# A mixture-of-experts gate in phases: two blocks in the last phase instead of four, three in the first instead of one

## The chip, the cores and the metric

The kernel runs on one core of a Trainium2 chip. The metric is the device time of one execution in microseconds (us). Engines are named as in the profile: PE (TensorE), DVE (VectorE), ACT (ScalarE), POOL (GpSimd), SP (SyncE, which here only issues DMAs). Each engine takes its instructions in order.

## What is computed

One layer of a graph network and one feed-forward layer, on 6250 nodes of 256 numbers, with 100,000 edges:

```
Wh    = layernorm(x) @ W + b, two heads of 128
e     = leaky_relu(s[src] + t[dst]), s and t linear in Wh
x     = x + softmax-weighted sum of Wh[dst] over the edges of each src
xf    = layernorm(x);  Hd = gelu(xf @ W1 + b1)              (1024 wide)
probs = softmax(Hd @ Wg + bg)                               (8 experts)
x     = x + max(probs) * (Hd @ Wd[argmax] + bd[argmax])
```

Every node uses the one expert that its gate finds likeliest.

## The kernel before

Nodes are worked in 49 blocks of 128 (the last, block 48, has 106). The first 105 us project the nodes, write their rows to a table in DRAM and sort the edges.

**The edge stage** then takes a block every three slots of a written-out plan. For each block POOL issues 15 gathers of 128 table rows (`fetch`, L800), in three parts of five; DVE weighs them (`weigh`, L832), ACT copies the weights (L833), PE sums them (`add_up`, L840), and `finish` divides, adds x and takes mean and variance. Before that, `window`, `measure`, `split`, `choose` and `spread` find the block's edges; `spread` sends a small table through DRAM (`lrow`, `lbc`) with two DMAs on SP.

**The gate stage** works on four blocks at a time, a phase. `blocks_of(k)` says which blocks phase k has: phase 0 has block 0, phase 1 blocks 1 to 4, and so on, to phase 12 with blocks 45 to 48. A phase is normed (`g_norm`, `g_xn`), turned (`g_turn`), taken through the hidden layer in four parts (`g_hidden`, L923, with Gelu on ACT, L925), the logits (`g_logits` L961, `g_logits_out` L967, `g_fold` L973), the softmax and choice on DVE (`g_bias`, `g_max`, `g_exp`, `g_choose`), a count on PE (`g_count`, L1020 and L1021) and the places on DVE (`g_place`). `g_rows` turns the hidden rows back (L1044, copied by ACT, L1045), `g_rest` adds the node's x and gate, and `g_send` has POOL scatter the block's rows of 1282 numbers into `by_expert` in DRAM, a list for each expert (L1066).

**The list stage** takes full tiles of 128 rows of one expert, called entries here. `tabulate` makes a table on DVE of which tiles they are; `w_load` has SP load one (L1132), `w_turn` turns it on PE (L1044 again), `w_expert` multiplies it by the expert's weights (L1150 for the bias, L1152), `w_out` scales and adds on DVE (L1166). The results of most phases are put off: `w_wait` writes them to DRAM, and at the end `late_load` (SP) and `late_send` (POOL, L1183) bring them to the output. Those of the last two phases go straight to the output (`w_send`, POOL, L1190). Phase 12 has 14 entries, 55 in all; 37 are put off. Lists that are read while later rows are still sent lag by 512 rows (`LAG`).

**What sets the order.** `at(slot, place, fn, ...)` puts a step into a plan; it is sorted by slot, then place, then order of entry, and the steps are emitted in that order under a manual schedule. So each engine's queue has the order of the plan. Block b has its slots around 3b, phase k starts at u[k] = 3 * (its last block) + 5: 137 for phase 11, 149 for phase 12. Waits are derived from the tiles that a step reads and writes; `by_expert` is one tensor, and a load of it waits for the scatters that come before it in the plan. Buffers come from pools: three PSUM buffers `pf`, four `row` buffers and four `wg` buffers in SBUF, which `room` lends to rows late in the run, two `y` buffers. `hT`, which holds the hidden rows of a phase, exists once. Nine fills of the lists with empty rows (L614) stand in the plan at slots 26, 38, ... 122.

Of the kernel before, what the change touches and what calls it, by code (L numbers as in the profile page):

```python
# [36 lines left out]
def common_path(  # L37
# [36 lines left out]
    NB = -(-N // P)  # L74
# [17 lines left out]
    TW = H * D2  # L92
    SE = D2 + D
    FB = 4
    NPH = -(-(NB - 1) // FB) + 1
    G = P // 4

    RW = C + 4
# [70 lines left out]
    def rows_of(b):  # L169
        return min(P, N - b * P)  # L170
# [16 lines left out]
    with ExitStack() as edges:  # L187
# [3 lines left out]
        def at(slot, place, fn, *args):  # L191
            plan.append((slot, place, len(plan), fn, args))
# [225 lines left out]
        def scales(b0, b1):  # L418


            n = b1 - b0
            r = rs[:, b0:b1]
            ve = sp.tile([P, NB], F32, name="n1ve")[:, :n]
            gi = sp.tile([P, NB], I32, name="n1gi")[:, :n]
            sq = sp.tile([P, NB], F32, name="n1sq")[:, :n]
            g = gi.bitcast(F32)
            yield nc.vector.tensor_scalar(ve, mv[:, b0:b1, 1], EPS, None, op0=ALU.add)
            yield nc.vector.tensor_single_scalar(gi, ve.bitcast(I32), 1, op=ALU.logical_shift_right)
            yield nc.vector.tensor_scalar(gi, gi, -1.0, float(0x5F375A00), op0=ALU.mult, op1=ALU.add)
            for it in range(3):  # L430
                yield nc.vector.tensor_mul(sq, g, g)
                yield nc.vector.scalar_tensor_tensor(sq, sq, -0.5, ve, op0=ALU.mult, op1=ALU.mult)
                yield nc.vector.scalar_tensor_tensor(r if it == 2 else g, sq, 1.5, g,
                                                     op0=ALU.add, op1=ALU.mult)
# [79 lines left out]
        for i, (d, flip) in enumerate(steps):  # L514
            t = 11 + 1.7 * i if i < 18 else 41.6 + 1.02 * (i - 18)
# [16 lines left out]
        for f0, f1, t0, step in ((n0, n1, 8.0, 0.7), (n4, NB - 1, 15, 2.0)):  # L532
            for j, b in enumerate(range(f0, f1)):
                c = b % CH
                t = t0 + step * (j - 0.5 * c)
# [7 lines left out]
        for c0, c1, t in ((0, n0, 0.27), (n0, n2, 15), (n2, n4, 31), (n4, NB, 58.5)):  # L543
            todo = scales(c0, c1)
            for i in range(12):
                early(t + (0.001 if c0 == 0 else 0.12) * i, next, todo, None)
        for b in range(NB):
            t = XN0 + NODE * b
# [67 lines left out]
        win, kept, rows, own, sums, res = {}, {}, {}, {}, {}, {}  # L616
# [226 lines left out]
        def finish(b):  # L843
            kept.pop(b)
            r = rows_of(b)
            k = -(-b // FB)
            i = b - blocks_of(k)[0]
            if i == 0:
                res[k] = {"rows": fw.tile([P, FB, RW], F32, name="res"),
                          "mom": fw.tile([P, FB, 2], F32, name="mom")}  # L850
                if blocks_of(k)[-1] == NB - 1 and N % P:
                    nc.vector.memset(res[k]["rows"], 0.0)
                    nc.vector.memset(res[k]["mom"], 0.0)
            o = res[k]["rows"][:r, i, :]
            xo = own.pop(b)[:r]
            p_a = sums.pop(b)
            den = ep.tile([P, H], F32, name="den")
            nc.vector.tensor_scalar(den_all[:r, b, :], p_a[:r, D:D2], TINY, None, op0=ALU.max)
            nc.vector.reciprocal(den[:r], den_all[:r, b, :])
            for h in range(H):  # L860
                hs = slice(h * D, (h + 1) * D)
                nc.vector.scalar_tensor_tensor(o[:, hs], p_a[:r, h * D2:h * D2 + D], den[:r, h:h + 1], xo[:, hs],
                                               op0=ALU.mult, op1=ALU.add)
            st = ep.tile([P, 6], F32, name="st2")
            nc.vector.bn_stats(st[:r], o[:, :C])
            nc.vector.bn_aggr(res[k]["mom"][:r, i, :], st[:r])
# [15 lines left out]
        put_off, late_y = [], {}  # L882
        put_off_idx = fc.tile([P, 2 * PAIRS], I32, name="put_off_idx")
# [41 lines left out]
                nc.scalar.activation(hT[:, j, :w], ph[:, :w], AF.Gelu, bias=wt["b1"][:, j:j + 1])  # L925

        def blocks_of(k):
            return range(max(0, (k - 1) * FB + 1), min(NB, k * FB + 1))

        def g_norm(k):  # L930
            bs = blocks_of(k)
# [108 lines left out]
        def turn_half(o, rows, h):  # L1040

            pT = pff.tile([P, 512], F32, name="pf")
            for j in range(4):
                nc.tensor.transpose(pT[:, j * P:(j + 1) * P], rows(4 * h + j), ident)  # L1044
            nc.scalar.copy(o, pT)  # L1045

        def room(late):

            if not late:
                return fw.tile([P, RD], F32, name="row", bufs=4)  # L1050
            return gp.tile([P, HT, TW], F32, name="wg").rearrange("p t c -> p (t c)")[:, :RD]

        def g_rows(k, i):

            row = res[k]["row", i] = room(k == NPH - 1 and i > 1)
            for h in range(2):
                turn_half(row[:, h * 512:(h + 1) * 512], lambda j: hT[:, j, i * P:(i + 1) * P], h)

# [68 lines left out]
        def w_load(k, i):  # L1127
            sr = res[k]["sr", i] = room(k == NPH - 1 or k == NPH - 2 and i in (2, 3))
            _, ro = nc.values_load_multi_w_load_instructions(
                res[k]["where"][0:1, i:i + 1], engines=[SP], min_val=0, max_val=SPARE,  # L1130
                skip_runtime_bounds_check_because="a tile of a list, or the spare tile")
            nc.sync.dma_start(out=sr, in_=by_expert[ds(ro[0], P), :])  # L1132
# [23 lines left out]

        def w_out(k, i):
            sr = res[k].pop(("sr", i))
            idx = res[k]["idx", i] = (put_off_idx[:, len(put_off):len(put_off) + 1] if k < NPH - 2 else
                                      fw.tile([P, 1], I32, name="idx"))  # L1160
            if "again" in res[k]:
                nc.vector.tensor_add(idx, sr[:, HID + C + 1:], res[k]["again"][:, i:i + 1])
            else:
                nc.vector.tensor_copy(idx, sr[:, HID + C + 1:])
            y = res[k]["y", i] = fw.tile([P, C], F32, name="y", bufs=2)
            nc.vector.scalar_tensor_tensor(y, res[k].pop(("py", i))[:, :C], sr[:, HID + C:HID + C + 1],  # L1166
                                           sr[:, HID:HID + C], op0=ALU.mult, op1=ALU.add)
# [28 lines left out]
        for b in range(NB):  # L1196
            u = 3 * b
# [27 lines left out]
        worked = n_off = 0  # L1225
        u = [3 * blocks_of(k)[-1] + 5 for k in range(NPH)]
        for k in range(NPH):
            bs = blocks_of(k)
            v = u[k]
            last = k == NPH - 1  # L1230
            at(v, 34 if last else 51, g_norm, k)
            for i in range(-(-len(bs) // 2)):
                at(v + 0.5 * i, 52, g_xn, k, i)
                at(v + 1, 38 + 0.1 * i, g_turn, k, i)
                at(v + 1, 45 + 0.1 * i, g_turned, k, i)
            for q in range(4):
                at(v + 2 + q, 20, g_hidden, k, q)
            at(v + 6, 19, g_logits, k)
            at(v + 6, 56, g_logits_out, k)
            at(v + 7, 36, g_fold, k)  # L1240
            at(v + 8, 12, g_bias, k)
            at(v + 8, 35 if last else 51, g_max, k)
            at(v + 8, 58, g_exp, k)
            at(v + 9, 35 if last else 51, g_choose, k)
            at(v + 10, 36, g_count, k)
            at(v + 11, 35 if last else 51, g_place, k)
            for i in range(len(bs)):
                t, p = (((v + 6, 40), (v + 6, 41), (v + 8, 60), (v + 8, 61))[i] if last else
                        ((v + 10, 38), (v + 11, 38), (v + 13, 38), (v + 13, 39))[i])
                at(t, p, g_rows, k, i)  # L1250
                at(max(t, v + 10), p, g_rest, k, i)
                at(v + 14 if i > 1 and not last else v + 12, 44, g_send, k, i)
            rows_in = min(N, (bs[-1] + 1) * P)
            n = (TILES if last else max(0, (rows_in - LAG) // P)) - worked
            worked += n
            if n == 0:
                continue
            assert n <= NMAX
            n_off += n if k < NPH - 2 else 0
            todo = tabulate(k, n, last)  # L1260
            for i in range(2):
                at(*((v + 12, 35) if last else (v + 12 + 3 * i, 53)), next, todo)
            for i in range(n):
                t = v + 15 + i if last else u[k + 1] + (5 + 8 * i // n if k < NPH - 2 else (7, 10, 11, 12, 13)[i])
                at(t - 1 if last else t - 2 if k == NPH - 2 else max(t - 3, v + 15), 46 if last else 64, w_load, k, i)
                at(t, 21, w_turn, k, i)
                at(t + 1, 22, w_expert, k, i)
                at(t + 2, 11 if k < NPH - 2 else 36, w_out, k, i)
                at(t + 2, 45, w_send if k >= NPH - 2 else w_wait, k, i)
        at(v + 18, 47, judge)  # L1270
        for j in range(-(-n_off // 2)):
            t = 3 * NB + 3 + j + (7 if j > 9 else 0)
            at(t - 2, 66, late_load, j)
# [537 lines left out]
```

## Time and profile before

| | us |
|---|---|
| median of three runs | 1725.15 (1710.7 to 1726.61) |
| the profiled execution | 1334.17 |
| its span, first to last instruction | 1332.0 |
| PE busy | 1124.3 (84%) |
| DVE busy | 1081.0 (81%) |
| POOL busy | 878.3 (66%) |
| ACT busy | 509.3 (38%) |
| mean granted PE clock | 0.935 |

The profile is of one execution, and its instructions' times are on that execution's scale; the runs shown took longer. POOL's busy time leaves out the 0.30 us in which each of its DMAs is issued. One fp32 matmul is two records on PE, so that a tile's expert multiplication (eight matmuls) shows as x16. A timeline row gives start, duration, engine, line, operation, output and inputs, and in brackets the idle time before it with what ended it.

### The profile page before, as it was taken

The numbers are of one execution on the slowest core, as the hardware profiler recorded it, in microseconds if no ns is written. First come the engines' busy times: TensorE is split into PE (matmuls) and PEld (weight loads), VectorE is DVE, ScalarE is ACT, GpSimd is POOL, SyncE is SP. The second block draws the span as 40 slices with busy tenths as digits, with TensorE's granted clock in tenths as the row PEclk, the third lists the DMA queues.
The fourth block names the chain that finished last, engine by engine and source line by source line (L and its number), as shares of the span: only waits on it lengthen the run. The fifth ranks groups of instructions, "written<-read, shape, count | busy, mean of one in ns | idle before, by whom it ended". The sixth has DMA issues, their size and how long they took to land. (4 is left out here: it accounts for less than half of the span.)

```text
span 1332.0 us, 22104 instructions
## 1 busy us (share of the span) xinstructions
PE 1124.3 (84%) x6405; PEld 858.8 (64%) x6405; DVE 1081.0 (81%) x3765; ACT 509.3 (38%) x1424; POOL 878.3 (66%) x989
## 2 busy tenths in 40 slices
PE   4783677887987989989989899899897998989697
PEld 3562466556665776766867667668576686775585
DVE  6995899898998998999999999989999998862011
ACT  4772222323424334344352443433434434344121
POOL 1004777777777777777777777777777777736262
PEclk9796897897988998999999999899999998999799
DMA  4754776666666766666666766666667666746572
GB/s 137 237 189 128 211 216 196 190 203 192 183 178 189 215 207 199 193 224 208 211 214 200 225 209 207 214 206 178 216 191 235 200 201 200 228 162 231 182 258 70
DMA packets 119212, 264.22 MB, mean 198 GB/s; under 512 B 24988, under 2 KB 65076, under 8 KB 118940
## 3 DMA queue, kind: packets, MB, share of 16 engines
q0 software_dynamic: 47264, 137.46, 34.2%
q1 hardware_dynamic: 64544, 118.23, 27.9%
q10 hardware_dynamic: 7276, 7.03, 1.6%
q8 instruction: 55, 0.90, 0.3%
q14 instruction: 73, 0.60, 0.1%
HBM read 211.45 MB, written 57.90 MB: 202 GB/s over the span
## 5 line engine op out<-in xcount | busy, mean ns | idle before, releaser
L800 POOL DMA_INDIRECT wg<-table,dsti x735 | 715.4, 973 | 225.3 <-issue 188.2
L840 PE MATMUL p_a<-wg,hot 128*128 128x258 f32 x1470 | 382.2, 411 | 73.6 <-ACT wg L833 73.6
L840 PEld LDWEIGHTS p_a<-wg,hot 128*128 128x128 f32 x1470 | 294.4, 206 | 133.6 <-ACT wg L833 80.3
L832 DVE TENSOR_TENSOR wg<-wg,fix 128x1280 f32<-128x1280 f32 x147 | 218.9, 1489 | 5.1
L1152 PE MATMUL pf<-wd_sb,half 128*128 x880 | 205.3, 386 | 0.0
L923 PE MATMUL pf<-xT,w_sb 128*128 128x512 f32 (+1 forms) x416 | 188.5, 599 | 7.4 <-ACT xT L915 7.4
L1152 PEld LDWEIGHTS pf<-wd_sb,half 128*128 128x128 f32 x880 | 163.2, 190 | 37.8 <-issue 14.7
L833 ACT COPY wg<-fix 128x10 f32<-128x10 f32 x147 | 24.7, 168 | 329.8 <-DVE wg L832 273.2
L923 PEld LDWEIGHTS pf<-xT,w_sb 128*128 128x128 f32 x416 | 77.2, 201 | 86.3 <-issue 72.9
L710 ACT ACTIVATE wt<-tm,hot_e 128x128 f32<-128x128 f32 x392 | 125.0, 392 | 1.7 <-PE p_a L725 1.7
L817 DVE TENSOR_TENSOR hot<-fix,loc 128x640 f32<-128x640 f32 x147 | 120.0, 816 | 0.0
L925 ACT ACTIVATE hT<-pf,b_sb 128x512 f32<-128x512 f32 (+1 forms) x104 | 68.4, 662 | 71.8 <-PE pf L923 71.0
L1045 ACT COPY half<-pf 128x512 f32<-128x512 f32 x110 | 61.3, 588 | 82.4 <-PE pf L1044 49.7
L1045 ACT COPY row<-pf 128x512 f32<-128x512 f32 x94 | 52.3, 586 | 94.7 <-PE pf L1044 93.9
L450 PE MATMUL pf<-w_sb,xT 128*128 128x260 f32 x196 | 60.3, 436 | 18.1 <-ACT xT L444 18.1
L1044 PE MATMUL pf<-ident,hT 128*128 128x128 f32 x392 | 59.7, 286 | 18.0 <-ACT row L1045 13.1
L622 POOL DMA_INDIRECT win<-keys,first x49 | 48.9, 999 | 32.1 <-DMA keys<-keyb 14.2
L1066 POOL DMA_INDIRECT by_expert<-row,place_i x47 | 47.4, 1008 | 32.1 <-ACT half L1045 11.6
L771 ACT CAST lT<-pm 15x128 bf16<-15x128 f32 x49 | 12.4, 253 | 141.7 <-PE pm L769 141.7
L1044 PEld LDWEIGHTS pf<-ident,hT 128*128 128x128 f32 x392 | 45.3, 145 | 30.1 <-ACT row L1045 17.9
L1166 DVE SCALAR_TENSOR_TENSOR y<-pf,wg 128x256 f32<-128x256 f32 x16 | 7.7, 484 | 59.7 <-PE pf L1152 59.7
L725 PEld LDWEIGHTS p_a<-hot_x,wt 128*128 128x128 f32 x392 | 51.9, 200 | 6.2 <-issue 5.7
(274 smaller groups left out, 1760.0 us busy)
## 6 DMA issues: line engine op xcount, KB each, us to landing
row<-by_expert SPq DMA_DIRECT2D x39, 641.0 KB
lbc<-lrow SPq DMA_DIRECT2D x49, 480.0 KB
tm<-terms SPq DMA_DIRECT2D x49, 256.0 KB
wg<-table,dsti POOLq DMA_INDIRECT x735
wg<-by_expert SPq DMA_DIRECT2D x16, 641.0 KB
wd_sb<-in_L_ffn_Wd_dram SPq DMA_DIRECT2D x8, 1024.0 KB
table<-tb ACTq DMA_DIRECT2D x12, 520.0 KB
xs<-in_x_dram SPq DMA_DIRECT2D x12, 512.0 KB
```

What stands on the lines that cost most here:

```text
L450: nc.tensor.matmul(pW[:, :TW], xT[:, k * P:(k + 1) * P], w_sb[:, k, :], start=(k == 0), stop=(k == KC - 1))
L710: nc.scalar.activation(kept[b]["wt"][:, i, g, h, :], tm[:, i, h, :], AF.Identity, scale=hot_e[:, g, i, h:h + 1])
L725: nc.tensor.matmul(sums[b][:, hs], wt[:, 0, g, h, :], hot_x[:, g, hs], start=False, stop=False)
L800: nc.gpsimd.indirect_dma_start(out=wg[:, t - QS[q], :], out_offset=None, in_=table[:, :], in_offset=bass.IndirectOffsetOnAxis(ap=kept[b][" ...
L817: nc.vector.tensor_tensor(hot[:, :n], iota_ps.unsqueeze(1).to_broadcast([P, n, P]), kept[b]["loc"][:, QS[q]:QS[q + 1]].unsqueeze(2).to_bro ...
L832: nc.vector.tensor_mul(wgv[:, :, :, :D], wgv[:, :, :, :D], p_w.unsqueeze(3).to_broadcast([P, n, H, D]))
L840: nc.tensor.matmul(sums[b], hot[:, t - QS[q], :], wg[:, t - QS[q], :SE], start=(t == 0), stop=(t == T - 1))
L923: nc.tensor.matmul(ph[:, :w], wt["w1"][:, k, j * P:(j + 1) * P], xT[:, k, :w], start=(k == 0), stop=(k == KC - 1))
L925: nc.scalar.activation(hT[:, j, :w], ph[:, :w], AF.Gelu, bias=wt["b1"][:, j:j + 1])
L1044: nc.tensor.transpose(pT[:, j * P:(j + 1) * P], rows(4 * h + j), ident)
L1045: nc.scalar.copy(o, pT)
L1152: nc.tensor.matmul(py[:, :C], res[k]["half", i, j // 4][:, j % 4, :], wt["wd"][:, ds(wo[0] + j * C, C)], start=False, stop=(j == KH - 1))
```

## The change

The phases are cut from the other end: the last one has two blocks (47 and 48, 234 nodes in 256 columns), the first three (0 to 2), all others four. There are 13 phases as before. Each phase but the last starts six slots later; u[11] is 143, u[12] still 149.

With that, phase 11 now ends after the last block's edges. It is called `near` in the plan: its rows are turned at the slots that the last phase has for it, two of them into `wg` buffers; all four blocks are sent at slot 155; its table is made in one go at slot 155; its four entries are loaded at slots 156, 158, 160, 162 and turned at 158, 160, 162, 164. The last phase's steps after its turn are put one slot later (w = v + 1), since phase 11's are just ahead. The entries of phase 10, worked at slots 148 to 155, now go straight to the output as well (`k < NPH - 3` in place of `k < NPH - 2`), so 35 are put off. Phase 11 keeps four entries; the last phase has 12.

```
-    NPH = -(-(NB - 1) // FB) + 1
+    NPH = -(-(NB - 2) // FB) + 1
+    AHEAD = (2 - NB) % FB
...
-            k = -(-b // FB)
+            k = (b + AHEAD) // FB
...
-            return range(max(0, (k - 1) * FB + 1), min(NB, k * FB + 1))
+            return range(max(0, k * FB - AHEAD), min(NB, (k + 1) * FB - AHEAD))
...
-            row = res[k]["row", i] = room(k == NPH - 1 and i > 1)
+            row = res[k]["row", i] = room(k == NPH - 1 or k == NPH - 2 and i > 1)
...
-            idx = res[k]["idx", i] = (put_off_idx[:, len(put_off):len(put_off) + 1] if k < NPH - 2 else
+            idx = res[k]["idx", i] = (put_off_idx[:, len(put_off):len(put_off) + 1] if k < NPH - 3 else
...
-            last = k == NPH - 1
+            last, near = k == NPH - 1, k == NPH - 2
...
+            w = v + 1 if last else v
             for q in range(4):
-                at(v + 2 + q, 20, g_hidden, k, q)
-            at(v + 6, 19, g_logits, k)
+                at(w + 2 + q, 20, g_hidden, k, q)
+            at(w + 6, 19, g_logits, k)
...
             for i in range(len(bs)):
-                t, p = (((v + 6, 40), (v + 6, 41), (v + 8, 60), (v + 8, 61))[i] if last else
-                        ((v + 10, 38), (v + 11, 38), (v + 13, 38), (v + 13, 39))[i])
+                t, p = (((w + 6, 40), (w + 6, 41), (w + 8, 15), (w + 8, 16))[i] if last or near else
+                        ((w + 10, 38), (w + 11, 38), (w + 13, 38), (w + 13, 39))[i])
                 at(t, p, g_rows, k, i)
-                at(max(t, v + 10), p, g_rest, k, i)
-                at(v + 14 if i > 1 and not last else v + 12, 44, g_send, k, i)
+                at(max(t, w + 10), p, g_rest, k, i)
+                at(w + 14 if i > 1 and not last and not near else w + 12, 44, g_send, k, i)
...
-            n_off += n if k < NPH - 2 else 0
+            n_off += n if k < NPH - 3 else 0
             todo = tabulate(k, n, last)
             for i in range(2):
-                at(*((v + 12, 35) if last else (v + 12 + 3 * i, 53)), next, todo)
+                at(*((w + 12, 35 + i) if last or near else (w + 12 + 3 * i, 53)), next, todo)
             for i in range(n):
-                t = v + 15 + i if last else u[k + 1] + (5 + 8 * i // n if k < NPH - 2 else (7, 10, 11, 12, 13)[i])
-                at(t - 1 if last else t - 2 if k == NPH - 2 else max(t - 3, v + 15), 46 if last else 64, w_load, k, i)
+                t = w + 15 + i if last else u[k + 1] + ((9, 11, 13, 15, 15)[i] if near else 5 + 8 * i // n)
+                at(t - 1 if last else t - 2 if near else max(t - 3, w + 15), 46 if last else 64, w_load, k, i)
                 at(t, 21, w_turn, k, i)
                 at(t + 1, 22, w_expert, k, i)
-                at(t + 2, 11 if k < NPH - 2 else 36, w_out, k, i)
-                at(t + 2, 45, w_send if k >= NPH - 2 else w_wait, k, i)
-        at(v + 18, 47, judge)
+                at(t + 2, 36 if last or near else 11, w_out, k, i)
+                at(t + 2, 45, w_send if k >= NPH - 3 else w_wait, k, i)
+        at(v + 19, 47, judge)
```

More of the change, by code (lines that the diff above doesn't have):

```diff
@@ L1235, in common_path @@
                 at(v + 1, 45 + 0.1 * i, g_turned, k, i)
+            w = v + 1 if last else v
             for q in range(4):
-                at(v + 2 + q, 20, g_hidden, k, q)
-            at(v + 6, 19, g_logits, k)
[L1239 to L1246, printed above, removed]
+                at(w + 2 + q, 20, g_hidden, k, q)
+            at(w + 6, 19, g_logits, k)
+            at(w + 6, 56, g_logits_out, k)
+            at(w + 7, 36, g_fold, k)
+            at(w + 8, 12, g_bias, k)
+            at(w + 8, 35 if last else 51, g_max, k)
+            at(w + 8, 58, g_exp, k)
+            at(w + 9, 35 if last else 51, g_choose, k)
+            at(w + 10, 36, g_count, k)
+            at(w + 11, 35 if last else 51, g_place, k)
             for i in range(len(bs)):
-                t, p = (((v + 6, 40), (v + 6, 41), (v + 8, 60), (v + 8, 61))[i] if last else
-                        ((v + 10, 38), (v + 11, 38), (v + 13, 38), (v + 13, 39))[i])
+                t, p = (((w + 6, 40), (w + 6, 41), (w + 8, 15), (w + 8, 16))[i] if last or near else
+                        ((w + 10, 38), (w + 11, 38), (w + 13, 38), (w + 13, 39))[i])
                 at(t, p, g_rows, k, i)
-                at(max(t, v + 10), p, g_rest, k, i)
-                at(v + 14 if i > 1 and not last else v + 12, 44, g_send, k, i)
+                at(max(t, w + 10), p, g_rest, k, i)
+                at(w + 14 if i > 1 and not last and not near else w + 12, 44, g_send, k, i)
             rows_in = min(N, (bs[-1] + 1) * P)
```

## The prediction

> **What bounds the kernel now.** I read the page's slices first, then POOL's timeline in the middle of the run, then PE's timeline and the chain that ended last in the tail, and last the busy time by stage there.
>
> Between about 115 and 1171 us it is POOL. In the slices of the page its busy digit stands at 7 all the way, and that is its ceiling: the timeline shows why.
>
> ```profile
> POOL 1004777777777777777777777777777777736262
> ```
>
> ```profile
> 859.44 0.98 POOL L1066 DMA_INDIRECT by_expert<-row,place_i  x1 [0.30 <-ACT wg L833]
> 860.42 0.09 POOL L895 MEMSET idle<- 1x1 f32 x1
> 860.73 0.98 POOL L1066 DMA_INDIRECT by_expert<-row,place_i  x1 [0.23 <-issue]
> 862.01 1.44 POOL L800 DMA_INDIRECT wg<-table,dsti  x1 [0.30 <-issue]
> 863.76 0.96 POOL L800 DMA_INDIRECT wg<-table,dsti  x1 [0.30 <-issue]
> 865.03 0.95 POOL L800 DMA_INDIRECT wg<-table,dsti  x1 [0.30 <-issue]
> ...
> 1170.22 0.95 POOL L800 DMA_INDIRECT wg<-table,dsti  x1 [0.30 <-issue]
> ```
>
> A gather of 0.95 us starts every 1.25 us, with 0.30 us before it that nothing explains but issuing; a pair of row sends (L1066) costs 862.01 - 859.44 = 2.57 us. The last of 735 gathers starts at 1170.22. After that the edge stage has one block left to weigh and add, and PE ends it at 1185.04 (call this F). What follows is the tail, 1185 to 1332, and there the order of PE decides:
>
> ```profile
> 1182.86 2.34 PE L840 MATMUL p_a<-wg,hot 128*128 128x258 f32 x10
> 1196.61 15.59 PE L923 MATMUL pf<-xT,w_sb 128*128 128x512 f32 x32 [1.95 <-ACT xT L915]
> 1237.73 3.72 PE L1152 MATMUL pf<-wd_sb,half 128*128 x16
> 1252.28 3.85 PE L1044 MATMUL pf<-ident,wg 128*128 128x128 f32 x16 [10.83 <-DMA wg<-by_expert]
> ```
>
> The chain that ended last says what filled the hole before 1252:
>
> ```profile
> 1225.69 0.04 PE pf L1021
> 1228.25 0.96 POOL by_expert L1066
> 1234.06 14.14 DMA by_expert<-wg,place_i
> 1248.39 3.75 DMA wg<-by_expert
> 1314.60 3.65 PE pf L1152 x16
> ```
>
> So from F: 40.65 us to the last phase's counting matmul (1225.69), 8.37 to its last row send (1234.06), 14.2 until that lands, 4.05 until the first list entry is in SBUF (1252.28), then 14 entries in 69.8 us to 1322.1, together F + 137.1. The kernel ends 10 us later. A list entry in steady state is 0.87 + 0.21 + 3.65 = 4.74 us of PE (turn, bias, expert).
>
> What the landing waits for is read from the busy time by stage:
>
> ```profile
> 1228.00:1234.00 6.00, 4.85 (x27) 4.05 (x27) 5.07 (x29) 1.30 (x3) 3.13 (x6) 1.00 0.71 282
> 1244.00:1248.00 4.00, 0.00 (x0) 0.00 (x0) 0.00 (x0) 0.00 (x0) 0.00 (x0) 0.53 0.12 51
> ```
>
> The last columns are the granted clock, the DMA share and GB/s. While the sends of full blocks drain, 282 GB/s move; in the last 4 us it is 0.12 of the 16 DMA engines, two of them, at 51 GB/s.
>
> **What the Trainium skill says.** "DMA: Bandwidth & Descriptors", section "Why a DMA increments its semaphore by 16 and not by 1": a DMA is spread over the largest number of engines up to 16 that divides its slowest dimension. Block 48 has 106 rows, 2 x 53, so two engines; the 0.12 agrees, and 106 rows of 5128 bytes took 14.14 us. This decides one term below: the landing is that of block 48, however many blocks are sent with it. "TensorE: Matmul & The Clock Gate", Part 1: PE falls to half clock after an idle window of some 3.4 us. The trace agrees: clock 0.53 in the hole, then 16 transposes in 3.85 us against 1.93 when warm. "ScalarE: Activation LUTs", "What ACT_TABLE_LOAD costs": 1283 ns for a switch; the trace has 1.28 us, and the tail keeps its Gelu and Exp switches, so no change.
>
> **The change part by part.** Blocks 43 to 46 become the phase before last (11), blocks 47 and 48 the last (12); the first phase has blocks 0 to 2.
>
> *POOL before F.* All sends up to phase 10 are placed ahead of the last gathers: 41 blocks before, 43 after. POOL has no slack there (its timeline from 115 to 1171 us has three gaps of more than 0.6 us, 2.9 us together), so the last gather starts 2.57 us later. What follows it need not keep its length: before, L833 of the last gather waited on ACT behind row copies of phase 11 that are now later. In exchange PE must fit the four quarters of phase 11's hidden layer (3.65 us each) between the last blocks' sums. Counting slots 145 to 148 on PE: 14.6 hidden, 4 sums x 2.2, two pairs x 1.06, one turn 1.3 = 26.9 us, from about 1158-1160 (before, the sum of block 47's second part ended at 1157.9), gives 1185 to 1187. Bounds for F: -1.3 (PE on time) to +2.6; I take **+1**.
>
> *PE from F to the last counting.* Phase 10's four entries now have slots 148 to 155, so they lie after F; before, only one expert of phase 10 did. PE in its new order: logits 11 1.9; expert 10.0 3.9; rows of two blocks, four halves. Each half needs a PSUM buffer (pf has three; the logits and py hold two), so at worst they alternate with ACT at 1194.00 - 1192.64 = 1.36 us a half: 5.4. On two buffers, as for rows 1213.98 to 1216.5 now, they take 2.5; I keep both ends and take 5.4. Turn 10.1 with fold 11 behind the lgT copy, and the turn of phase 12: 3.8, to F + 15.0. Rows of the other two blocks 2.5; expert 10.1 3.9. Hidden 12 is 256 wide: 32 records at the 0.228 us of a 256-wide L1152 = 7.3 (before 15.6, a gain of 8.3); between its quarters turns 10.2 and 10.3, 2.0, and experts 10.2 and 10.3, 7.8; count 11 0.2. Logits 12 0.95, rows 2.5, fold with its copy 1.5. Sum F + 43.7. So the 8.3 + 0.9 of logits + 2.5 of rows that the last phase loses are paid back by three entries (14.2), logits and fold of phase 11, and a row more.
>
> *A new wait.* Next on PE is turn 11.0 (slot 158), and behind it in PE's order stand expert 11.0, turn 11.1 and only then count 12 (slot 160). Entry 11.0 can be loaded when all four sends of phase 11 have landed. From count 11: 2.56 to the first send (as 1225.69 to 1228.25), four blocks of 656 KB at 282 GB/s = 9.3 plus 2 for the end of a transfer, load 4.05: 18.0 us. PE gets there 13.5 us after count 11 (q2 1.83, turn 1.0, q3 1.83, expert 3.9, then 4.95 as above). Stall **4.5**; bounds 0 (PE late) and about 11 (the four sends land as the 106-row one did). Then turn with its copy 1.6, expert 3.9, turn 1.1, and 0.1: count 12 at F + 54.9, against 40.65.
>
> *Sends and landing.* Two sends instead of four: 2.56 to the first and 1.28 to the second. Before, block 48's own send started 2.3 us late (1231.8 to 1234.06) for a reason the page does not give; I keep it (bounds 0 and 2.3): F + 61.1, where 49.0 was. Landing 14.14 and load 4.05 unchanged: F + 79.3. The tables of phase 12 wait in DVE's order for entry 11.1, done 4.4 us after count 12, hidden under the landing. In that hole PE has expert 11.1, turn and expert 11.2, 9.4 us; then it idles some 15 us, colder than before. Entry 11.3 is no filler: its load (slot 162, place 46) stands behind the sends of phase 12 (162, 44), reads the same DRAM tensor, and so waits for them.
>
> *The entries at the end.* 13 (11.3 and twelve) instead of 14: 69.8 - 4.74 = 65.1. End F + 144.4, against F + 137.1: +7.3. With F: **+8.3 us**. The other moves cost nothing: late loads and sends on SP and POOL have until the 13 entries end (before, the last was at 1301), two fewer put-off entries, the opening phase lies under POOL's back-to-back gathers.
>
> The profiled execution took 1334.17 us with a span of 1332.0; it would become 1342.5. The median of the runs shown is 1725.15, 1.29 times as much; the profile does not show where the other 391 us are. I add the difference as it is, **1733**; stretched by 1.29 it would be 10.7.
>
> **Rivals.** *The smaller phase pays.* Rows pass on two buffers (-2.9), PE reaches turn 11.0 after the list has landed (-4.5), block 48's send is not held (-2.3), F comes early (-2.3): -3.7, 1721. For it: each is within its bound; against: all four at once. *The lists land late.* The stall is 11 instead of 4.5, F is +2.6: +16.4, 1741. For it: before, the first load of phase 11 left SP 9.1 us after its fourth send, not 7.5. *SP's queue.* The fills of by_expert (L614) sit at slots 2 modulo 12. Phases now end six slots later, so the first list load falls on that very slot just ahead of the fill, the second just behind. A load was followed by the fill after 5.5 us (563.00 to 568.53); then the second load waits some 4 us more, and lrow for the next block stands behind it. Moved by a slot of 7.3 us, that ends at about 580.4, where lrow left at 580.20: on the edge. If it passes it, DVE's compare, which waits up to 2.4 us for lbc already, holds the gathers' buffers: 8 fills x 2.4 = 19 more, +27, 1752. Against it: DVE is 91% busy and can catch up 8 us a phase. *Nothing comes of it*: losses and gains cancel, 1725.
>
> **How the numbers follow.** Main case 0.48 (1733, own range 1724 to 1742); smaller phase pays 0.18; late lists 0.12; SP's queue 0.15; nothing 0.07. The range of 8 in 10 leaves out the far half of the SP case and the best of the first rival: 1714 to 1750, the 16 us spread of the runs before included. A run of this kernel tells 1% from no change at best. Faster by over 1% needs -17, which not even all good ends give: 0.05. Slower by over 1% needs +17: SP's queue, half of the late lists and a stretched main case, 0.24. Same 0.71.
>
> **What would show it.** Right: PE idle before the first turn of phase 11 waiting for a DMA; count 12 some 55 us after F; a hole of over 12 us before entry 11.3; 13 turns and experts in a row after it; the last gather 2 to 3 us later. Wrong: no idle before 11.0, a fill of the hole by 11.3, a landing well under 14 us, or POOL gaps in the middle of the run.

## The result, and the profile after

The changed kernel took 1750.66 us (median of four, 1746.29 to 1753.66) where the kernel before took 1725.88 (1710.7 to 1736.11): 1.0143 times as long, 95% interval 1.0098 to 1.0187, or 24.8 us more. The forecast was 1733, 8 us more, with 1750 as the upper end of its range.

In these runs both kernels take about 1.3 times as long as on the three chips of the experiments below and as in the profile of the kernel before, for a reason that no run shows (the record gives no chip for them), so the two profiles are not set against each other, and the experiments compare kernels on one chip each.

The profile of the changed kernel has a span of 1751.6 us. POOL in the slices of its page:

```profile
POOL 0034655546555655554554554646555546542533
```

The digit is 4 to 6 where it was 7, so in this execution POOL is not working gather behind gather. The tail has the predicted form all the same. First PE's timeline, then the chain that ended last, then busy time by stage (the last columns are clock, DMA share and GB/s):

```profile
1590.39 2.34 PE L842 MATMUL p_a<-wg,hot 128*128 128x258 f32 x10
1653.42 0.17 PE L1023 MATMUL pf<-oh,ones_bf 128*128 128x16 bf16 x1
1675.63 1.94 PE L1046 MATMUL pf<-ident,wg 128*128 128x128 f32 x8 [12.25 <-DMA wg<-by_expert]
1738.22 3.72 PE L1154 MATMUL pf<-wd_sb,half 128*128 x16
```

```profile
1657.50 14.19 DMA by_expert<-wg,place_i
1672.61 5.52 DMA wg<-by_expert
```

```profile
1660.00:1666.00 6.00, 3.38 (x16) 2.64 (x14) 3.11 (x18) 0.10 (x1) 1.49 (x4) 0.98 0.26 76
1666.00:1671.00 5.00, 0.00 (x0) 0.00 (x0) 0.00 (x0) 0.00 (x0) 0.00 (x0) 0.50 0.16 63
```

(Lines are two further down than in the kernel before: its L1044, the turn, is L1046.) F, the end of PE's last edge sum, is taken as before, 2.18 us after the start of the last L842: 1592.6. The count of the last phase follows at F + 60.9, the send of block 48 takes 14.19 us to land, PE then has stood still for 12.25 us, and thirteen turns and experts end at F + 149.2. This end is taken 3.56 us after the start of the last L1154, where in a row of entries the next instruction begins, and so in every profile below; by this measure the profile of the prediction has F + 136.9, where the prediction wrote 137.1.

### The profile page after: what moved, and what is told of

Its sections match the earlier page's. It is cut to its first block, busy times and chain, and to the rows that moved or that the text cites. A ratio compares the mean times of both kernels' runs of the same rounds, so it can differ in the third digit from the quotient of the medians.

```text
span 1751.6 us, 22103 instructions
## 1 busy us (share of the span) xinstructions
PE 1269.3 (72%) x6405; PEld 948.7 (54%) x6405; DVE 1085.5 (62%) x3765; ACT 510.1 (29%) x1424; POOL 873.3 (50%) x989
## 4 chain that ended last, share of the span: by engine, by line
PE 37%; DVE 29%; another core or an unknown queue 14%; issue 9%; ACT 6%; DMA 4%; POOL 0%; SPq 0%; ACTq 0%; DVEq 0%; POOLq 0%
PE pf L925 9%; PE p_a L842 8%; PE pf L1154 7%; DVE wg L834 5%; PE pf L1046 4%; DVE hot L819 3%; PE p_a L727 2%; PE pm L698 1%; PE pf L963 1%; ACT xnf L904 1%; ACT wt L712 1%; PE pm L748 1%; ACT row L1047 1%; PE pm L789 1%
## 5 line engine op out<-in xcount | busy, mean ns | idle before, releaser
L842 PE MATMUL p_a<-wg,hot 128*128 128x258 f32 x1470 | 392.8, 420 | 54.4 <-ACT wg L835 37.5
L842 PEld LDWEIGHTS p_a<-wg,hot 128*128 128x128 f32 x1470 | 303.8, 213 | 120.8 <-ACT wg L835 44.3
L1154 PE MATMUL pf<-wd_sb,half 128*128 x880 | 229.6, 408 | 23.5 <-issue 19.8
L834 DVE TENSOR_TENSOR wg<-wg,fix 128x1280 f32<-128x1280 f32 x147 | 218.9, 1489 | 10.6 <-DVE fix L833 5.3
L925 PE MATMUL pf<-xT,w_sb 128*128 128x512 f32 (+2 forms) x416 | 218.8, 675 | 6.5 <-ACT xT L917 3.8
L1154 PEld LDWEIGHTS pf<-wd_sb,half 128*128 128x128 f32 x880 | 170.5, 201 | 77.3 <-issue 49.4
L796 DVE TENSOR_REDUCE fs<-pm 128x60 f32<-128x180 f32 x49 | 16.9, 346 | 287.9 <-remote 112.8
L925 PEld LDWEIGHTS pf<-xT,w_sb 128*128 128x128 f32 x416 | 91.7, 232 | 99.9 <-issue 87.4
L1046 PE MATMUL pf<-ident,hT 128*128 128x128 f32 x392 | 71.7, 326 | 81.8 <-ACT row L1047 60.0
L927 ACT ACTIVATE hT<-pf,b_sb 128x512 f32<-128x512 f32 (+2 forms) x104 | 68.3, 662 | 211.9 <-PE pf L925 65.1
L1068 POOL DMA_INDIRECT by_expert<-row,place_i x45 | 44.1, 979 | 164.0 <-ACT row L1062 64.9
L1046 PEld LDWEIGHTS pf<-ident,hT 128*128 128x128 f32 x392 | 54.4, 167 | 93.7 <-ACT row L1047 66.0
L835 ACT COPY wg<-fix 128x10 f32<-128x10 f32 x147 | 24.8, 169 | 254.6 <-DVE wg L834 119.4
L1046 PE MATMUL pf<-ident,row 128*128 128x128 f32 x328 | 55.2, 314 | 47.5 <-ACT half L1047 27.8
L727 PE MATMUL p_a<-hot_x,wt 128*128 128x129 f32 x392 | 73.1, 337 | 11.6 <-issue 11.1
L727 PEld LDWEIGHTS p_a<-hot_x,wt 128*128 128x128 f32 x392 | 67.5, 246 | 24.3 <-issue 23.1
```

The source lines that it names most:

```text
L727: nc.tensor.matmul(sums[b][:, hs], wt[:, 0, g, h, :], hot_x[:, g, hs], start=False, stop=False)
L834: nc.vector.tensor_mul(wgv[:, :, :, :D], wgv[:, :, :, :D], p_w.unsqueeze(3).to_broadcast([P, n, H, D]))
L842: nc.tensor.matmul(sums[b], hot[:, t - QS[q], :], wg[:, t - QS[q], :SE], start=(t == 0), stop=(t == T - 1))
L925: nc.tensor.matmul(ph[:, :w], wt["w1"][:, k, j * P:(j + 1) * P], xT[:, k, :w], start=(k == 0), stop=(k == KC - 1))
L1068: st = nc.gpsimd.indirect_dma_start(out=by_expert[:, :], out_offset=bass.IndirectOffsetOnAxis(ap=place_i[:r, i:i + 1], axis=0), in_=row[:r ...
L1154: nc.tensor.matmul(py[:, :C], res[k]["half", i, j // 4][:, j % 4, :], wt["wd"][:, ds(wo[0] + j * C, C)], start=False, stop=(j == KH - 1))
```

## The experiments

All differences below are of medians, against the kernel before on the same chip in the same runs, where it took 1338 to 1341 us.

**Both kernels unchanged, side by side on one chip.** The kernel before, against itself:

> The kernel before, unchanged: a control, and above all a second profile of it. The profile shown (span 1332 us) is not of the kind of the timed runs (about 1725 us), while the profile of the changed kernel (1751.6 us) is. Tail theory (the added time lies after the last edge sum): this profile has its last edge sum within 3 us of the changed kernel's 1592.6 us, and a tail from there to the last expert matmul of 125 to 142 us against the 149 us there. Edge-stage theory (the added time is lost while the blocks are summed): its last edge sum is 10 us or more earlier than 1592.6. Third possibility: this profile shows 1332 us again, and then the two regimes have to be explained first.

Measured: 1.5 us apart, ratio 1.0009 (0.9987 to 1.0031). It was the third possibility: the new profile has a span of 1344.2 us. The changed kernel:

> The changed kernel, unchanged, beside the kernel before on one chip: ratio 1.010 to 1.019 as measured. Tail theory: 12 to 25 us of it after the last edge sum. Edge-stage theory: 12 to 25 us of it before.

Measured: 1372.29 against 1338.15, 34.1 us more, ratio 1.0254 (1.0176 to 1.0332), so more than expected. In the two profiles F is 1216.2 against 1196.8, and the last expert multiplication ends 141.5 us after F against 137.3. So 19.4 of the 23.6 us between the two spans are lost before F, in the edge stage that the forecast had left untouched but for 1 us. How much is known only roughly from one profile each: F of the kernel before was 1185.0 in the profile of the prediction and is 1196.8 here. Gather 225 (counted from 0) starts at 430.0 in the changed kernel and at 436.3 in the kernel before, gather 675 at 1116.0 and 1094.0: the loss lies between them, some 4 us a phase.

**The load of entry 11.3 ahead of the last sends.** The forecast said that this entry could not fill the hole because its load stands behind the sends of phase 12.

```
-                at(t - 1 if last else t - 2 if near else ...
+                at(t - 1 if last else t - 2 - i // 3 if near else ...
```

> The changed kernel with the load of the fourth entry of the phase before last moved from slot 162 to 161, so that it stands ahead of the last phase's two row sends and need not wait for them. Theory that this wait adds an entry to the end: the entry fills the hole before the last phase's entries, 12 entries follow the hole and not 13, and the time falls by 4 to 5 us against the changed kernel. If the hole is bounded otherwise (DVE or SP late), no change.

Measured: 28.6 us over the kernel before, 5.5 under the changed kernel; the intervals (1.0155 to 1.0254 and 1.0176 to 1.0332) overlap. The profile lets no 4 us be seen: the turn of 11.3 moves into the hole, its expert stays behind the turn of entry 12.0 in PE's order, and the end is F + 140.4 instead of 141.5. The step as it was tried is worth about 1 us.

**The fills where they stood.** What keeps its slot while the phases move is only the fills of the lists (L616 here).

```
-            at(26 + 12 * (NX - e), 80, lambda e=e: nc.sync.dma_start(out=by_expert[...], in_=empty))
+            at(32 + 12 * (NX - e), 80, lambda e=e: nc.sync.dma_start(out=by_expert[...], in_=empty))
```

> After, with the nine fills of the lists moved six slots later, so that they stand to the phases as they did before. Theory SP's queue: the 19.4 us that the changed kernel had lost by its last edge sum (1216.2 against 1196.8 in two profiles of one chip) come from the fill that stands between the first and the second list load of a phase; they go, and what stays is the tail's 4 us and the 1 us of two more sends: 3 to 9 us over the kernel before, and the last edge sum within 3 us of it. Rival, the opening phase or the new order of rows and sends costs the time: no change from the changed kernel, 25 to 34 us over the kernel before.

Measured: 8.0 us over the kernel before, ratio 1.0050 (1.0027 to 1.0074); F in its profile is 1199.9. Then the other way round, the kernel before with its fills moved (the first of them left in place, as the loads of the first phase need it):

```
-            at(26 + 12 * (NX - e), 80, ...)
+            at(26 + 12 * (NX - e) + (6 if e < NX else 0), 80, ...)
```

> Before, with its fills moved six slots later (but for the first of them), onto the slot of the first list load of a phase, and nothing else changed. SP's queue: 14 to 24 us slower than before, all of it ahead of the last edge sum; DVE's waits for lbc grow from 11 to 20 us or more in the stretch 430 to 1120 us. Rival: no change, within 4 us.

Measured: 24.6 us slower than the kernel before, ratio 1.0147 (1.0076 to 1.0218), with nothing of the change in it; F at 1212.4, the end 138.9 after it. The granted clock is no explanation: its median over the runs is 0.932, and 0.934 in the kernel before beside it. DVE's waits between 430 and 1120 us:

```profile
DVE lbc L779 <- DMA lbc<-lrow: 29.2, 8, 4.8
```

(In all, times, longest.) They were 11.3 us in seven in the last profile of the kernel before. The fills' place is enough to make the loss, and without it the loss is gone.

**The same pair on one chip, and no fills in the steady part.** The two runs of the changed kernel so far were on different chips. So both again, beside a third in which the nine fills are made early:

```
-            at(26 + 12 * (NX - e), 80, ...)
+            at(4 + 1.5 * (NX - e), 80, ...)
```

> The changed kernel again, on the same chip as the two runs beside it. 25 to 35 us over the kernel before where the kernel before takes about 1340; if it takes about 1725 there, 20 to 30 over it.

> The changed kernel with its fills six slots later, beside the changed kernel. The fills' place: 15 to 27 us under the changed kernel, 5 to 12 over the kernel before. If the chip is one on which the kernel before takes about 1725, the second list load there leaves 9 to 10 us ahead of lrow, and the fills then should cost less: 0 to 15 us under the changed kernel, and the rest has another cause.

> The changed kernel with all nine fills in slots 4 to 16, so that none is left in the steady part. If a fill costs only by standing between two list loads: as with the fills six slots later, within 4 us of it. If every fill costs something wherever it stands in the steady part: 5 us or more faster than with the fills six slots later.

Measured, against 1339.4: the changed kernel 1372.46 (+33.1, ratio 1.0226, 1.0152 to 1.0299), with fills six slots later 1346.32 (+6.9, 1.0056, 1.0033 to 1.0080), with early fills 1346.23 (+6.8, 1.0057, 1.0032 to 1.0081). The fills' place costs 26.1 us, and fills that stand well cost nothing that shows. How it does so is read from SP's timeline of the changed kernel, around one phase's first load:

```profile
757.13 0.35 SPq L1134 DMA_DIRECT2D row<-by_expert  x1
761.25 0.52 SPq L616 DMA_DIRECT2D by_expert<-empty  x1
761.86 0.53 SPq L810 DMA_DIRECT2D own<-in_x_dram  x1
762.49 1.68 SPq L703 DMA_DIRECT2D tm<-terms  x1
766.21 0.34 SPq L1134 DMA_DIRECT2D row<-by_expert  x1
769.38 0.37 SPq L775 DMA_DIRECT2D lrow<-lT  x1
772.48 0.34 SPq L777 DMA_DIRECT2D lbc<-lrow  x1
```

and with the fills six slots later:

```profile
744.47 0.35 SPq L1134 DMA_DIRECT2D row<-by_expert  x1
744.92 0.38 SPq L810 DMA_DIRECT2D own<-in_x_dram  x1
745.41 0.37 SPq L703 DMA_DIRECT2D tm<-terms  x1
746.28 0.34 SPq L1134 DMA_DIRECT2D row<-by_expert  x1
756.68 0.37 SPq L775 DMA_DIRECT2D lrow<-lT  x1
758.80 0.33 SPq L777 DMA_DIRECT2D lbc<-lrow  x1
```

In the first the fill waits 4.1 us until the load ahead of it has landed, and the second load waits until the fill has: it leaves 9.1 us after the first load where the others leave 1.8 us apart, and only 3.2 us before `lrow`. `lrow` itself is not late in SP's queue (12.2 us after the first load in both), but its 3.8 KB are: `lbc`, which waits for them, follows after 3.1 us and in the other phases after up to 4.4, where the kernel before has 1.4 to 2.6 for the same block, once 3.1. Then DVE, and behind it POOL. Waits of both between 430 and 1120 us in the changed kernel, and below with the fills six slots later:

```profile
DVE lbc L781 <- DMA lbc<-lrow: 23.7, 8, 3.6
POOL by_expert L1068 <- issue: 17.8, 26, 2.8
POOL wg L802 <- ACT wg L835: 17.1, 11, 4.5
```

```profile
DVE lbc L781 <- DMA lbc<-lrow: 6.4, 8, 1.1
POOL by_expert L1068 <- issue: 9.5, 26, 2.8
POOL wg L802 <- ACT wg L835: 1.8, 6, 0.3
```

POOL loses 17.1 - 1.8 = 15.3 us to gather buffers that come free late, and 17.8 - 9.5 = 8.3 us ahead of its row sends, for which the profile names no releaser ("issue"); from gather 225 to gather 675 it takes 685.4 us instead of 659.7, 25.7 more. In the slices:

```profile
POOL 0005777777777776777767777777677677626262
```

```profile
POOL 1004777777777777777777777777777777726162
```

The first line is of the changed kernel, the second with the fills moved: the sixes are where gathers were lost.

**Which part of the fills' place.** If only the late second load matters, it could be moved out of the way of `lrow`:

```
-                at(... max(t - 3, w + 15), 46 if last else 64, w_load, k, i)
+                at(... max(t - 3, w + 15 + 2 * (i == 1)), 46 if last else 64, w_load, k, i)
```

> After, fills where the change leaves them, but the second list load of each phase two slots later, so that lrow and lbc of the next block are issued ahead of it. If what costs is the chain load, fill, load in SP's queue with lrow and lbc behind it, most of the loss ahead of the last edge sum goes: 5 to 14 us over the kernel before, where the changed kernel is 34 over it. If the fill's own 641 KB or the wait of SP for the first load to land is what costs, the chain being no part of it: 25 to 34 us over the kernel before.

Measured: 38.9 us over the kernel before (ratio 1.0274, 1.0177 to 1.0371): nothing was gained, a miss. DVE's waits:

```profile
DVE fs L796 <- PE pm L698: 21.7, 10, 4.0
DVE lbc L781 <- DMA lbc<-lrow: 12.9, 7, 2.4
```

The wait for `lbc` is back near the 11.3 us of the kernel before, as the theory had it, but another has grown: DVE's wait for PE's factors (L789), which is 8.7 us in the changed kernel, too small to be listed with the fills moved, and 21.7 here. The turn of the second entry stands ahead of the factors in PE's order and has its load later; PE is seen to wait there for a `row`, but in only two places, 5.0 us, so that this is the likely cause and no more. The run thus does not tell the two theories apart. A second try left the loads alone and put the fill behind the second of them:

```
-            at(26 + 12 * (NX - e), 80, ...)
+            at(27 + 12 * (NX - e), 80, ...)
```

> After, with the fills one slot later than the change leaves them, that is behind the second list load of a phase and no longer between the first and the second. The earlier run that moved the second load instead did not get the time back, but it made PE wait for that load. Theory, it is the second load that leaves late, held by the fill, and its transfer that lrow then queues behind: the second load is again some 10 us ahead of lrow, lrow takes 1.4 to 2.3 us as before where it took 3.2 to 4.7, and the kernel is 3 to 12 us over the kernel before. Rival, what costs is that a fill and two list loads fall into one slot of a block, in whatever order: 20 to 34 us over the kernel before.

Measured: 14.7 us over the kernel before, ratio 1.0116 (1.0065 to 1.0166), between the two expectations. The second load is again 10.2 to 11.1 us ahead of `lrow`, but now the fill is 2.4 to 4.0 us ahead of it, and `lbc` follows `lrow` after 1.9 to 3.3 us. So most of the loss goes with the second load being late. In this profile gathers 225 to 675 take 666.7 us, no more than the 666.9 in the profile with the fills six slots later on this chip; where the rest lies (14.7 against 8.0 us in the medians), and whether the fill just ahead of `lrow` makes it, is not shown.

Set side by side, the profiles bear out that the loss passes through DVE. DVE's waits for `lbc` and for PE's factors are added here (430 to 1120 us) and put beside the time from gather 225 to gather 675:

| us | DVE's two waits | POOL's stretch |
|---|---|---|
| changed, fills six slots later | 6.4 | 659.7 |
| changed, fills one slot later | 16.6 | 666.7 |
| changed (beside the first) | 32.4 | 685.4 |
| changed, second load two slots later | 34.6 | 689.5 |
| before | 12.6 | 657.6 |
| before, fills moved | 36.5 | 677.1 |

Against the first line POOL's stretch grows by 25.7 us where the two waits grow by 26.0, by 29.8 for 28.2, and by 7.0 for 10.2; in the kernel before by 19.5 for 23.9. So moving the second load seems to have traded one of DVE's waits for the other. In the changed kernel the second wait also follows from the first: at 778.45 us PE's turn of an entry waited 1.44 us for a DVE step (L1168) that stands just behind the compare with `lbc`, and the factors stand behind that turn. This is a match over six profiles; no run changed DVE's order alone.

**The order in the tail.** In the changed kernel the last count stands behind the turn of entry 11.0, which waits for its list. Here the four entries of phase 11 are turned behind the count, and all their loads stand ahead of the last sends:

```
-                t = ... u[k + 1] + ((9, 11, 13, 15, 15)[i] if near else ...)
-                at(t - 1 if last else t - 2 if near else ...
+                t = ... u[k + 1] + (11.5 + i if near else ...)
+                at(t - 1 if last else (w + 13, w + 15, w + 17, w + 18)[i] if near else ...
```

> After, with only the tail's order changed: the four entries of phase 11 are turned from slot 160.5 on, one a slot, behind the last counting instead of ahead of it, and all four loads stand ahead of the last two sends. Theory, the order put the count behind a wait for a list: the count comes some 14 us earlier from the last edge sum (39 to 42 us after it instead of 53.6), the hole of 12 us before the last entries is filled by the four entries, end 122 to 130 us after the last edge sum instead of 141.5; 11 to 19 us faster than the changed kernel. Rival, the landing of the last sends is held by something else and moves with the lists: the hole stays, within 5 us of the changed kernel.

Measured: 24.0 us over the kernel before (1.0117 to 1.0255), 10 under the changed kernel in the median; in the profile F comes 3 us earlier, which is less than F differs between profiles of one kernel, and the end is F + 139.7 instead of 141.5, so the tail has won 2 us, not 11 to 19. The count comes at F + 44.1, 9.7 earlier, but the first entry of phase 12 is turned at F + 77.8, where it was F + 78.6. The chain says why:

```profile
1259.53 8.25 DMA wg<-by_expert
1267.85 3.14 issue
1272.44 14.38 DMA by_expert<-wg,place_i
1287.82 5.12 DMA wg<-by_expert
```

The places were known at 1258.9, yet the first send left at 1271.2: the sends write the tensor that the four loads ahead of them read, and the last of those landed at 1267.8 (the 3.1 us after that are put down to issuing). The wait for lists went from PE's order into the sends.

**128 rows in the last send.** The Trainium skill, "DMA: Bandwidth & Descriptors", section "Why a DMA increments its semaphore by 16 and not by 1", lets a transfer use the largest number of engines up to 16 that divides its slowest dimension: two for 106 rows, sixteen for 128. In the kernel before, 22 rows more are sent to places 106 to 127, ahead of where the first list begins:

```
+            if rows_of(blocks_of(k)[-1]) < P:
+                nc.vector.tensor_add(place[:, nb - 1:nb], place[:, nb - 1:nb], pad)
...
-            r = rows_of(blocks_of(k)[i])
+            r = P
```

(`pad` is the row number from row 106 on, else zero; the tokens of these rows are past the last node, so nothing of them reaches the output.)

> Before, with the last block's send made of 128 rows instead of 106; the 22 rows more go to places that nothing reads. Theory, 106 rows are spread over two DMA engines and 128 over sixteen: the landing of 14.1 us falls to 3 to 6, the hole of 10.8 us before the first list entry shrinks to 0 to 3, 7 to 11 us faster than before. Rival, the landing takes its time for being the last of four sends and for what lies between a transfer's end and the next issue: within 3 us of before.

Measured: 1327.4 against 1339.48, 12.1 us faster than the kernel before, ratio 0.9882 (0.9825 to 0.9940). The landing in the chain:

```profile
1241.15 6.86 DMA by_expert<-wg,place_i
1249.09 5.78 DMA wg<-by_expert
```

6.86 us instead of 14.1, a little over the 3 to 6 expected; the hole is 3.16 us and one of 0.97, and the end F + 128.9 instead of 137.3. So 8.4 of the 12.1 us lie in the tail, and the rest is within what F differs between profiles. In the tail, too, block 48's send no longer leaves 2.2 us late, as it did in the kernel before. The DMA share (next to last) says that it is no longer two engines that work while the sends land:

```profile
1243.00:1247.00 4.00, 4.00 (x19) 3.19 (x18) 0.48 (x1) 0.59 (x1) 0.45 (x2) 1.00 0.79 303
```

It is 0.79 of the sixteen, at 303 GB/s, against 0.12 and 51 in the kernel before. Two variants on this, first the kernel before with the early fills too:

> Before, with the 128-row send and all nine fills in slots 4 to 16, ahead of the first list load. If the fills cost also where the kernel before has them (SP waits 34 us for them, DVE 11 us for lbc): 4 to 11 us faster than with the 128-row send alone, 16 to 23 faster than before. If they cost nothing there: 10 to 14 faster than before, as with the 128-row send alone; less, if they now collide with the loads of the experts' weights.

Measured: 11.0 us faster than before, ratio 0.9899 (0.9832 to 0.9966). No cost of the fills shows where the kernel before has them; the interval, 5 to 23 us faster, makes the 16 to 23 of the other expectation unlikely and does not exclude it. Then the changed kernel with fills six slots later and 128 rows, in its own tail order:

> After, with the fills six slots later and 128 rows in the last block's send, and the tail's order as the change has it. The landing falls by 7 us and the hole before entry 11.3 by as much: end 135 to 138 after the last edge sum, within 4 us of the kernel before; the tail's order is then worth the 5 to 10 us by which the run with all three edits is faster. If the two-block phase is better in itself once sends land fast: 5 us or more faster than before, and the order worth nothing.

Measured: 2.3 us under the kernel before, ratio 0.9975 (0.9952 to 0.9997), end F + 135.6. And with the new tail order as well:

> After, with three edits together: fills six slots later, the tail's order of the earlier experiment (entries of phase 11 behind the last counting), and 128 rows in the last block's send. If the smaller last phase pays once its sends land in 7 us and not 14: the hole before its list entries goes (0 to 2 us), end 129 to 134 us after the last edge sum, 3 to 8 us faster than before. If the sends wait again for the four list loads ahead of them and that is what sets the end: 137 or more after the last edge sum, 0 to 5 us slower than before.

Measured: 10.6 us under the kernel before, ratio 0.9932 (0.9896 to 0.9968), end F + 128.0, no hole. With these shorter landings the order is worth some 8 us (7.6 between the two tails), where with one of 14 the tail gained 2. Three kernels here are some 11 us faster than the kernel before; the smallest edit, 128 rows in the kernel before, is as fast as any.

## Why the prediction was wrong

**The step that failed** is "The other moves cost nothing", together with the weight of the rival named *SP's queue*. The rival had the right place (the fill on the slot of the first list load) and the right first consequence (the second load leaves late). It was held at 0.15 for two reasons. One was that the delay ended about where `lrow` left, "on the edge"; that was so in SP's queue, but what `lrow` writes then reached `lbc` 1 to 3 us later, phase by phase, than with the fills moved. The other was that DVE, 91% busy, "can catch up 8 us a phase". DVE may; POOL cannot. It issues a gather every 1.25 us with no slack, as the forecast's first paragraph had shown, so what it loses to a late buffer is not regained: 26.0 us more of DVE's waits went with 25.7 us more over the same gathers. POOL gaps in the middle of the run, which the prediction had named as a sign of being wrong, are what the profiles show. The estimate of 2.4 us for each of 8 fills, 19 in all, was low: 26.1 us, 3.3 a fill, in the changed kernel.

**F otherwise.** Two more sends, +1: with the fills moved the whole kernel is 6.9 to 8.0 us over the kernel before, and the tail takes 5 to 8 of it. The term is not shown by itself, since F differs by 12 us between two profiles of the kernel before, but little room is left for it.

**PE to the last counting.** F + 54.9 was forecast; nine profiles with this order on the three chips have F + 53.7 to F + 55.5, the profile of the result F + 60.9. The detailed order of entries, rows and hidden quarters held.

**The new wait.** 4.5 us was forecast ahead of the turn of entry 11.0. PE's timeline of the changed kernel beside the moved fills:

```profile
1218.77 2.34 PE L842 MATMUL p_a<-wg,hot 128*128 128x258 f32 x10
1266.28 1.94 PE L1046 MATMUL pf<-ident,row 128*128 128x128 f32 x8 [5.23 <-DMA row<-by_expert]
1296.68 1.94 PE L1046 MATMUL pf<-ident,wg 128*128 128x128 f32 x8 [12.23 <-DMA wg<-by_expert]
```

5.23, and 5.0 to 6.0 in the others with this order, apart from the profile of the result, where this turn is not seen to wait. The four sends ahead of it had landed 9.8 us after the first of them left; 11.3 (9.3 plus 2) was forecast.

**Sends and landing.** The landing of 14.14 stayed: 14.09 to 14.19 in nine profiles. Block 48's send was forecast to be held 2.3 us as before; in the changed kernel it left 0.22 us after the other, so the first entry came at F + 75.7 (to 77.7 in the other profiles) rather than 79.3: that part of *the smaller phase pays* was right, the rest of that rival was not. The hole was 12.2 us there. Entry 11.3 did not fill it, as forecast.

**The entries at the end.** Thirteen, 65.7 to 67.7 us against 65.1. Seven profiles with this tail on the three chips end 141.5 to 145.2 us after F (forecast 144.4), three with that of the kernel before 136.9 to 138.9.

**The sum.** The main case said +8.3; with the fills taken out of the way the change costs 6.9 to 8.0. So the terms that were worked out were right in sum, to some degree by errors that cancel (the first entry earlier by 1.6 to 3.6 us, the entries longer by 0.6 to 2.6), and one that was set to zero cost three times as much. In the runs of the result the whole is 24.8 us, close to the +27 of the rival; but that its cause there is the same is not shown, and the profile speaks against the same route. The second load leaves 7.7 to 9.3 us after the first there too, yet 7 to 13 us ahead of `lrow`, since a slot takes 10 us; `lbc` follows `lrow` after 1.4 to 2.1 us, DVE is seen to wait for `lbc` only 3.9 us in four (540 to 1455 us), and POOL waits for much else. The kernel before has no profile from those runs, and no fill was moved in them, so what made the 24.8 us stays open.

## What to carry to other kernels

When steps of a plan move together, list those that stay: a transfer on a fixed slot can come to stand between two others that depend on it, and then it holds a queue for two landings. An engine that is busy without a gap has no later chance to catch up, so a wait of one of its suppliers can count in full even where that supplier has slack. Before the work of a last stage is made smaller, look at what its landing is made of: here 22 padding rows were worth more than the new division of phases.

## What the runs showed of the hardware

A write of 3.8 KB that was issued 1.1 to 3.7 us after a load of 641 KB on the same queue released its reader after 3.1 to 5.4 us (three runs, eight cases each), and after 1.4 to 2.7 us (once 3.1) when that load had left 10 us before it and nothing large in between. A scatter of 106 rows of 5128 bytes landed after 14.1 us with a DMA share of 0.12 in its last 4 us; one of 128 rows landed after 6.9 us behind three others, after 5.1 behind one. The send of the 106 rows also occupied POOL for 1.55 us, that of 128 for 0.95.
